# Sixteen-head attention on small tiles of TensorE: score halves on its rows, value groups on its columns, quotients taken transposed

## The chip, the cores and the metric

The kernel runs on one NeuronCore of a Trainium2 chip. A core has engines that run beside each other, each with its own in-order queue: TensorE (PE in the profile: matmuls, with PEld for the loads of its stationary operand), VectorE (DVE), ScalarE (ACT), GpSimd (POOL) and SyncE (SP, which issues DMAs). TensorE writes only to PSUM, whose banks hold 512 f32 columns on each of 128 partitions; the other engines read it from there. The metric is device time of one execution in microseconds; the median of several runs is compared.

## The reference: what is computed

A Flamingo-like block of four layers on x of shape (2, 1024, 256), with a context of 64 rows per batch. Each layer is a gated cross-attention to the context and a gated mixture of experts (8 experts, inner width 1024). Everything is f32. The change concerns the attention of layers L1 and L3, which have 16 heads of 16 columns. Cut to what matters (L3; L1 has a key mask that adds -10000 to masked scores in place of the full mask, and its keys are masked too):

```python
q = split_heads(query @ wq_kernel + wq_bias)          # (b, 16, 1024, 16)
k = split_heads(key @ wk_kernel + wk_bias)            # (b, 16, 64, 16)
v = split_heads(value @ wv_kernel + wv_bias)
scores = jnp.einsum('bhqd,bhkd->bhqk', q, k) / jnp.sqrt(jnp.float32(HD))
scores = jnp.where(m == 0, jnp.float32(-1000000000.0), scores)
attn = jax.nn.softmax(scores, axis=-1)
out = jnp.einsum('bhqk,bhkd->bhqd', attn, v)
return out @ wo_kernel + wo_bias                      # after joining the heads
```

The result is multiplied by a gate and added to x.

## The kernel before

The 2048 tokens stand in SBUF as 16 tiles of 128 tokens (`xs`), in four groups (`NG`) of four tiles (`TG`). The layers follow each other: `xattn0`, `moe0`, `middle`, the experts of L2, `heads_xattn(heads3)` for the attention of L3, the experts of L3. `middle` holds the attention of L1, its experts (`ffn1_group`) and the single-head attention of L2, group by group: the attention of L1 for groups 0 and 1 stands ahead of the experts of group 0; that for groups 2 and 3 is written after the experts of groups 0 and 1. A planner of the framework orders the instructions of each engine from the dependencies, so that attention and expert work are mixed in the engines' queues; it also makes the waits and hands out the buffers.

The class `Heads` does the attention of L1 and L3. `setup` makes two operands once: `kblk`, in which the scaled keys of eight heads (128 rows) stand block-diagonally against eight times 64 columns, and `vaug`, in which for each pair of heads the values stand in two column groups of 17: sixteen value columns and a column of ones, so that one matmul gives the weighted values and the sum of the weights together. Then for each group:

- `queries` makes `qT`, the transposed queries of the group's 512 tokens, in two chunks `c` of eight heads (L372, L373).
- `scores` takes one tile of 128 tokens: for each chunk one matmul (L386) with all 128 rows of `qT` as the stationary operand and 512 columns of `kblk` streaming gives the scores of eight heads in one PSUM bank. On DVE follow the mask (L394, in L3) or the added key bias, which moves the scores to SBUF (L401, in L1), the maximum of each head (L408) and the subtraction (L409). One exponential for all 1024 columns follows on ACT (L412).
- `values` transposes the weights on PE, two heads at a time (L425), ACT copies them to `pT` (`evac`, L145), and eight matmuls (L434) use `pT` as the stationary operand with 34 columns of `vaug` streaming. DVE takes 16 reciprocals a row (L442) and multiplies (L444).
- `output` transposes the result (L452), ACT copies it to `oT`, two matmuls with `wo` follow (L458, by the helper at L198), DVE adds to `xs` (L460), POOL adds the bias (L461).

`group` writes these for tile i, i-1 and i-2 in one turn of its loop (L466 to L472). PSUM buffers: in L3 and for group 0 of L1 there are two for transposes (`pt`), four for scores (`ps`) and two for the rest (`py`). For groups 1 to 3 of L1 the class `Both` (L1178) hands out the same two `py` buffers for all three uses, since the experts hold the other banks.

Of the kernel before, what the change touches and what calls it, by code (L numbers as in the profile page):

```python
# [8 lines left out]
F32 = mybir.dt.float32  # L9
# [8 lines left out]
P = 128  # L18
B, S, D = 2, 1024, 256
SK = 64  # L20
# [21 lines left out]
def kernel(ctx: ExitStack, tc: tile.TileContext, a: dict, out: bass.AP):  # L42
# [100 lines left out]
    def evac(i, dst, src):  # L143
        if i % 2:
            A.copy(dst, src)  # L145
        else:
            V.tensor_copy(dst, src)  # L147
# [143 lines left out]
    class Heads:  # L291
# [8 lines left out]
        def setup(self, psp, tag):  # L300

            pre, key_mask, full_mask = self.pre, self.key_mask, self.full_mask
            tmp = wpool.tile([P, 2048], F32, name="w")
            wk = tmp[:, :512].rearrange("p (c d) -> p c d", c=NC)
            wv = tmp[:, 512:1024].rearrange("p (c d) -> p c d", c=NC)
            nc.sync.dma_start(wk, a[f"{pre}_wk"])
            nc.sync.dma_start(wv, a[f"{pre}_wv"])
            self.wq, self.wo = (load_w256(held, f"{pre}_{n}", n) for n in ("wq", "wo"))

            kblk = self.kblk = held.tile([P, B, NC, P // HD, SK], F32, name="kblk")  # L310
            vaug = self.vaug = held.tile([P, B, H // 2, 2, HD + 1], F32, name="vaug")
            if key_mask is not None:
                km_u = held.tile([P, B * SK // 4], I32, name="km_u")
                nc.scalar.dma_start(
                    km_u, key_mask.rearrange("b k -> (b k)").partition_broadcast(P)
                )
                km = held.tile([P, B * SK], F32, name="km")
                V.tensor_single_scalar(km, km_u.bitcast(U8), 0.0, ALU.not_equal)
                self.kbias = held.tile([P, B * SK], F32, name="kbias")
                V.tensor_scalar(self.kbias, km, -1.0, 10000.0, ALU.add, ALU.mult)  # L320
            if full_mask is not None:
                m_w = wpool.tile([P, 2048], F32, name="w")
                m_i = m_w[:, : NT * SK].rearrange("p (t k) -> p t k", k=SK).bitcast(I32)
                nc.scalar.dma_start(
                    m_i, full_mask.rearrange("b (t p) k -> p (b t) k", p=P)
                )
                self.dropm = held.tile([P, NT, SK], U8, name="dropm")
                V.tensor_single_scalar(self.dropm, m_i, 0.0, ALU.is_equal)
            for c in range(NC):
                ps = psp.tile([P, 512], F32, name=tag)  # L330
                mm256(
                    ps[:, :P], lambda k: wk[:, k, c * P : (c + 1) * P], lambda k: ctxT[:, k, :]
                )
                kT = tmp[:, 1024 + c * P : 1024 + (c + 1) * P]
                V.tensor_scalar(
                    kT, ps[:, :P], cols[:, self.c_bk, c : c + 1], 1.0 / HD**0.5,
                    ALU.add, ALU.mult,
                )
                if key_mask is not None:
                    V.tensor_mul(kT, kT, km)  # L340
                for b in range(B):
                    V.tensor_mul(
                        kblk[:, b, c],
                        kT[:, b * SK : (b + 1) * SK].unsqueeze(1)
                        .to_broadcast([P, P // HD, SK]),
                        blkmask.unsqueeze(2).to_broadcast([P, P // HD, SK]),
                    )

            for b in range(B):
                ps = psp.tile([P, 512], F32, name=tag)  # L350
# [3 lines left out]
                V.tensor_mul(  # L354
                    vaug[:, b, :, :, 0:HD],
                    v2.rearrange("p (i j d) -> p i j d", j=2, d=HD),
                    halfmask.unsqueeze(1).unsqueeze(3).to_broadcast([P, H // 2, 2, HD]),
                )
# [19 lines left out]
        def scores(self, tt, pools):  # L378

            b, t = tt // (NT // B), tt % TG  # L380
            two, pss = pools["two"], pools["ps"]
            pr = two.tile([P, H, SK], F32, name="pr")
            HC = H // NC
            for c in range(NC):
                ps = pss.tile([P, 512], F32, name="ps_s")
                T.matmul(  # L386
                    ps,
                    lhsT=self.qT[:, c, t * P : (t + 1) * P],
                    rhs=self.kblk[:, b, c].rearrange("p j k -> p (j k)"),
                    start=True, stop=True,  # L390
                )
# [7 lines left out]
                prc = pr[:, c * HC : (c + 1) * HC, :]  # L399
                if self.key_mask is not None:  # L400
                    V.tensor_add(  # L401
                        prc, ps3,
                        self.kbias[:, b * SK : (b + 1) * SK].unsqueeze(1)
                        .to_broadcast([P, HC, SK]),
                    )
                    ps3 = prc
                mx = two.tile([P, HC], F32, name="mx")
                V.tensor_reduce(mx, ps3, AX.X, ALU.max)  # L408
                V.tensor_tensor(  # L409
                    prc, ps3, mx.unsqueeze(2).to_broadcast([P, HC, SK]), ALU.subtract  # L410
                )
            A.activation(pr, pr, AF.Exp)  # L412
            self.live[tt] = pr

        def values(self, tt, pools):

            b = tt // (NT // B)
            two, pt, py = pools["two"], pools["pt"], pools["py"]
# [10 lines left out]
                    )  # L429
                evac(1, pT[:, q4 * 4 : q4 * 4 + 4, :].rearrange("p i q -> p (i q)"), pst)  # L430
            pso = py.tile([P, 512], F32, name="ps_y")
            w = 2 * (HD + 1)
            for hp in range(H // 2):
                T.matmul(  # L434
                    pso[:, hp * w : (hp + 1) * w],
                    lhsT=pT[:, hp, :],
                    rhs=self.vaug[:, b, hp].rearrange("p a d -> p (a d)"),
                    start=True, stop=True,
                )
            po3 = pso[:, : (H // 2) * w].rearrange("p (h d) -> p h d", d=HD + 1)  # L440
            rs = two.tile([P, H], F32, name="rs")
            V.reciprocal(rs, po3[:, :, HD])  # L442
            o = two.tile([P, H, HD], F32, name="o")
            V.tensor_mul(o, po3[:, :, 0:HD], rs.unsqueeze(2).to_broadcast([P, H, HD]))  # L444
            self.live[tt] = o

        def output(self, tt, pools):
            two, pt, py = pools["two"], pools["pt"], pools["py"]
# [12 lines left out]
            G.tensor_add(xt, xt, self.bo)  # L461
# [864 lines left out]
```

## Time and profile before

| | us |
|---|---|
| three runs | 2466.1, 2443.22, 2464.13 (median 2464.13) |
| the profiled execution, whole | 2454.52 |
| its span, first to last instruction | 2452.7 |
| granted TensorE clock, mean of the span | 0.922 |

| stretch of the profiled execution | from, to (us) |
|---|---|
| L1 attention, group 0, by itself | 430 to 466 |
| L1 attention, group 1, with the experts of group 0 | about 480 to 520 |
| L1 attention, group 2, with the experts of group 1 | 806 to 850 |
| L1 attention, group 3, with the experts of group 2 | 1146 to 1190 |
| L3 attention, four groups | 2062 to 2206 |

The page gives busy time of each engine, then the chain of work that ended last, followed back from the last instruction, with each engine's share. A group of instructions is named by its line in the kernel, its engine, its tiles (what is written, an arrow, what is read) and its shape; for matmuls the shape of the stationary operand stands first (`128*34` would be 128 rows and 34 columns), then that of the streaming one. Busy time of TensorE covers the pipeline of overlapping matmuls, so the distance between starts tells more of a matmul's price than its duration.

### The profile page before, as it was taken

Reading aid. Unit: us, or ns where it says so; the run is one execution under the profiler, and the core shown is the slowest. Engines: PE = TensorE matmul, PEld = TensorE weight load, DVE = VectorE, ACT = ScalarE, POOL = GpSimd, SP = SyncE. Lnnn points to the kernel's source line nnn. Section 1 sums busy time; section 2 is a strip of 40 time slices with the busy share of each in tenths; the row PEclk is TensorE's granted clock in tenths of the full one; section 3 lists DMA queues with packets and bytes.
Section 4 is the critical chain, followed back from the end, with each engine's and each line's share of the span. In section 5 each row is a group of like instructions: output and inputs, shape, how many; then the busy total and the mean of one; then the engine's idle time right before and its main releaser. Section 6 shows DMA issues by size and latency. Waiting matters only on the chain.

```text
span 2452.7 us, 27852 instructions
## 1 busy us (share of the span) xinstructions
PE 2199.9 (90%) x10132; PEld 1787.2 (73%) x10132; DVE 1255.2 (51%) x2742; ACT 757.9 (31%) x1431; POOL 1072.5 (44%) x1229
## 2 busy tenths in 40 slices
PE   5558887899999999999999999999968996986997
PEld 3357775588888778887788887888856774565775
DVE  7851003676566765655865656566551116663111
ACT  1003332353333533334433334333311221330221
POOL 3316664236666346665366664666303320000331
PEclk9758998899999989999999999999958998875998
DMA  3018887012222123222132222222413543010442
GB/s 97 26 59 270 275 248 241 1 52 86 86 86 87 50 63 91 89 88 73 48 95 88 88 91 78 86 86 86 141 66 86 139 112 92 18 58 22 116 116 51
DMA packets 97544, 235.07 MB, mean 96 GB/s; under 512 B 13184, under 2 KB 41088, under 8 KB 86976
## 3 DMA queue, kind: packets, MB, share of 16 engines
q1 hardware_dynamic: 70880, 159.14, 20.3%
q0 software_dynamic: 21456, 68.92, 10.3%
q10 hardware_dynamic: 5072, 5.23, 0.6%
q8 instruction: 81, 1.33, 0.2%
q14 instruction: 55, 0.45, 0.1%
HBM read 211.10 MB, written 24.25 MB: 96 GB/s over the span
## 4 chain that ended last, share of the span: by engine, by line
PE 74%; DVE 11%; DMA 5%; POOL 3%; issue 2%; ACT 2%; POOLq 0%; ACTq 0%; DVEq 0%; SPq 0%
PE ps_b L1036 12%; PE ps_m L198 10%; PE ps_e L1036 8%; PE ps_a L1036 8%; PE ps_y L765 8%; PE ps_b L1081 6%; PE ps_a L1081 4%; PE ps_e L1081 4%; PE ps_y L198 3%; PE ps_y L434 2%; DMA xg<-hd,idx 2%; PE ps_m L704 1%; PE ps_tr L186 1%; DMA xd_L<-y_ff,idx 1%; PE ps_y L386 1%
## 5 line engine op out<-in xcount | busy, mean ns | idle before, releaser
L1036 PE MATMUL ps_b<-xsum,w 128*128 128x256 f32 x1536 | 388.2, 381 | 2.3 <-DVE c L1062 2.2
L1036 PEld LDWEIGHTS ps_b<-xsum,w 128*128 128x128 f32 x1536 | 289.7, 190 | 47.6 <-issue 4.6
L943 POOL TENSOR_TENSOR w<-w 128x256 f32<-128x256 f32 x192 | 140.8, 734 | 404.0 <-DMA w<-in_L_Wu_dram 174.6
L1036 PE MATMUL ps_a<-hT,w 128*128 128x256 f32 x1024 | 270.0, 384 | 0.7 <-DVE hT L147 0.6
L198 PE MATMUL ps_m<-xT,w 128*128 128x128 f32 (+2 forms) x1248 | 253.8, 364 | 11.8 <-DVE xT L147 11.7
L765 PE MATMUL ps_y<-w,mid 128*128 128x256 f32 (+1 forms) x1136 | 252.8, 379 | 0.0
L198 PEld LDWEIGHTS ps_m<-xT,w 128*128 128x128 f32 x1248 | 188.5, 200 | 71.9 <-DVE xT L147 19.3
L765 PEld LDWEIGHTS ps_y<-w,mid 128*128 128x128 f32 (+1 forms) x1136 | 206.6, 184 | 38.9 <-issue 2.7
L988 ACT COPY u<-ps_b 128x512 f32<-128x512 f32 (+1 forms) x192 | 98.9, 515 | 411.0 <-PE ps_b L1081 264.0
L1036 PEld LDWEIGHTS ps_a<-hT,w 128*128 128x128 f32 x1024 | 194.2, 193 | 31.2 <-issue 3.2
L772 POOL DMA_INDIRECT xd_L<-y_ff,idx x48 | 74.9, 1561 | 232.4 <-DVE y_ff L771 135.8
L770 DVE TENSOR_TENSOR y_ff<-ps_y,b 128x256 f32<-128x256 f32 (+1 forms) x48 | 20.3, 423 | 298.0 <-PE ps_y L765 298.0
L944 POOL TENSOR_TENSOR w<-w 128x256 f32<-128x256 f32 x192 | 166.9, 869 | 0.0
L946 POOL TENSOR_TENSOR w<-w 128x256 f32<-128x256 f32 x192 | 158.9, 827 | 14.7
L945 POOL TENSOR_TENSOR w<-w 128x256 f32<-128x256 f32 x192 | 164.8, 859 | 0.0
L1036 PE MATMUL ps_e<-xsum,w 128*128 128x256 f32 x512 | 134.4, 383 | 0.0
L1036 PE MATMUL ps_e<-hT,w 128*128 128x256 f32 x512 | 134.1, 382 | 0.0
L1081 PE MATMUL ps_b<-t,w 128*128 128x256 f32 x512 | 132.8, 384 | 0.0
L1081 PE MATMUL ps_a<-b,w 128*128 128x256 f32 x512 | 132.0, 379 | 0.0
L970 ACT COPY ps_b<-ps_a 128x512 f32<-128x512 f32 (+1 forms) x192 | 96.5, 502 | 109.5 <-DVE b L1066 63.5
L1098 POOL TENSOR_TENSOR m<-m,accT 128x256 f32<-128x256 f32 x60 | 71.7, 1195 | 124.1 <-ACT m L976 110.4
L145 ACT COPY xT<-ps_tr 128x128 f32<-128x128 f32 (+2 forms) x39 | 13.4, 344 | 355.7 <-PE ps_tr L748 289.4
(306 smaller groups left out, 3928.5 us busy)
## 6 DMA issues: line engine op xcount, KB each, us to landing
w<-in_L_Wg_dram SPq DMA_DIRECT2D x64, 512.0 KB, 4.1
w<-in_L_Wu_dram SPq DMA_DIRECT2D x64, 512.0 KB, 4.1
w<-in_L_Wd_dram SPq DMA_DIRECT2D x64, 512.0 KB, 3.7
w<-in_L_W_dram SPq DMA_DIRECT2D x32, 1024.0 KB, 4.9
xd_L<-xs SPq DMA_DIRECT2D x8, 512.0 KB, 2.9
hd_L<-h SPq DMA_DIRECT2D x8, 512.0 KB, 3.0
xs<-in_x_dram SPq DMA_DIRECT2D x4, 512.0 KB, 10.5
xd<-xs SPq DMA_DIRECT2D x4, 512.0 KB, 2.9
```

The costliest lines, as they stand in the source:

```text
L198: T.matmul(ps, lhsT=lhs(c), rhs=rhs(c), start=(c == 0), stop=(c == n - 1))
L765: T.matmul(ps[:w, :], lhsT=mid[:, f, at : at + w], rhs=w2[:, f, :], start=(f == 0), stop=(f == NF - 1),)
L772: G.indirect_dma_start(out=xd[:, :], out_offset=bass.IndirectOffsetOnAxis(ap=idx[:w, j0 + s : j0 + s + 1], axis=0), in_=y[:w, :], in_offse ...
L943: G.tensor_add(s[0], a21, a22)
L944: G.tensor_sub(s[1], s[0], a11)
L945: G.tensor_sub(s[2], a11, a21)
L946: G.tensor_sub(s[3], a12, s[1])
L970: A.copy(self.b, self.pa)
L988: A.copy(u2, self.b)
L1036: T.matmul(ps[:, q * 256 : (q + 1) * 256], lhsT=lhs[kind][:, q, :], rhs=xr[kind], start=(first and q == 0), stop=True, skip_group_check=True,)
L1081: T.matmul(ps, lhsT=wd[kind][:, q, :], rhs=m["rhs"][kind][:, q * 256 : (q + 1) * 256], start=(clear and q == 0), stop=True, skip_group_che ...
L1098: G.tensor_add(sb, sb, acc[:, i, j])
```

## The change

*Scores.* The two matmuls of a tile with all 128 rows become four with 64 rows each, one for each half `r` of the rows and chunk `c`. A half holds four heads, so only 256 columns of `kblk` stream. The results of half 0 go to one PSUM bank and those of half 1 to another, so a tile takes both banks at once. The softmax then runs over a half (both chunks) where it ran over a chunk. In L1 the key bias is added in place in PSUM. In L3 the subtraction is dropped: DVE takes the negated maximum, and ACT makes one exponential for each head, with that maximum as its bias.

*Values.* The operands change places: `vblk` (32 columns, two heads, no ones) is stationary and `pT` streams with 128 columns; four matmuls write four groups of 32 partitions of the same PSUM columns. The result comes out transposed. The sums of the weights come from the same matmuls with a new constant `halves` (ones for a head's half of the rows) as the stationary operand: 16 columns for each head hold the same sum. DVE takes reciprocals of 256 columns in two instructions and multiplies.

*Output.* Since the quotients are already transposed, the two transposes and the copy on ACT go.

```diff
+    halves = const.tile([P, 2, HD], F32, name="halves")
+    V.tensor_copy(halves, halfmask.unsqueeze(2).to_broadcast([P, 2, HD]))
...
-            vaug = self.vaug = held.tile([P, B, H // 2, 2, HD + 1], F32, name="vaug")
+            vblk = self.vblk = held.tile([P, B, H // 2, 2, HD], F32, name="vblk")
...
-                V.tensor_copy(
-                    vaug[:, b, :, :, HD],
-                    halfmask.unsqueeze(1).to_broadcast([P, H // 2, 2]),
                 )
...
+            prv = pr.rearrange("p (c r j) k -> p r c j k", c=NC, r=2)
             HC = H // NC
+            pair = [pss.tile([P, 512], F32, name="ps_s") for _ in range(2)]
             for c in range(NC):
-                ps = pss.tile([P, 512], F32, name="ps_s")
-                T.matmul(
-                    ps,
-                    lhsT=self.qT[:, c, t * P : (t + 1) * P],
-                    rhs=self.kblk[:, b, c].rearrange("p j k -> p (j k)"),
-                    start=True, stop=True,
-                )
-                ps3 = ps.rearrange("p (j k) -> p j k", k=SK)
+                for r in range(2):
+                    T.matmul(
+                        pair[r][:, c * 256 : (c + 1) * 256],
+                        lhsT=self.qT[r * 64 : (r + 1) * 64, c, t * P : (t + 1) * P],
+                        rhs=self.kblk[r * 64 : (r + 1) * 64, b, c, r * 4 : (r + 1) * 4]
+                        .rearrange("p j k -> p (j k)"),
+                        start=True, stop=True,
+                    )
+            for r in range(2):
+                ps3 = pair[r].rearrange("p (j k) -> p j k", k=SK)
+                ps4 = pair[r].rearrange("p (c j k) -> p c j k", c=NC, k=SK)
...
                 if self.key_mask is not None:
                     V.tensor_add(
-                        prc, ps3,
+                        ps3, ps3,
...
+                if self.full_mask is not None:
+                    V.tensor_reduce(mx, ps3, AX.X, ALU.max, negate=True)
+                    for j in range(HC):
+                        c, k = divmod(j, HC // NC)
+                        A.activation(
+                            prv[:, r, c, k], ps3[:, j], AF.Exp, bias=mx[:, j : j + 1]
+                        )
+                    continue
                 V.tensor_reduce(mx, ps3, AX.X, ALU.max)
                 V.tensor_tensor(
-                    prc, ps3, mx.unsqueeze(2).to_broadcast([P, HC, SK]), ALU.subtract
-                )
-            A.activation(pr, pr, AF.Exp)
+                    prv[:, r], ps4,
+                    mx.rearrange("p (c j) -> p c j", c=NC).unsqueeze(3)
+                    .to_broadcast([P, NC, HC // NC, SK]),
+                    ALU.subtract,
+                )
+            if self.full_mask is None:
+                A.activation(pr, pr, AF.Exp)
...
-            w = 2 * (HD + 1)
-            for hp in range(H // 2):
-                T.matmul(
-                    pso[:, hp * w : (hp + 1) * w],
-                    lhsT=pT[:, hp, :],
-                    rhs=self.vaug[:, b, hp].rearrange("p a d -> p (a d)"),
-                    start=True, stop=True,
-                )
-            po3 = pso[:, : (H // 2) * w].rearrange("p (h d) -> p h d", d=HD + 1)
-            rs = two.tile([P, H], F32, name="rs")
-            V.reciprocal(rs, po3[:, :, HD])
-            o = two.tile([P, H, HD], F32, name="o")
-            V.tensor_mul(o, po3[:, :, 0:HD], rs.unsqueeze(2).to_broadcast([P, H, HD]))
-            self.live[tt] = o
+            for at, den in ((D, True), (0, False)):
+                for c in range(NC):
+                    for i in range(4):
+                        w = halves if den else self.vblk[:, b, c * 4 + i]
+                        T.matmul(
+                            pso[i * 32 : (i + 1) * 32, at + c * P : at + (c + 1) * P],
+                            lhsT=w.rearrange("p a d -> p (a d)"),
+                            rhs=pT[:, c * 4 + i, :],
+                            start=True, stop=True, skip_group_check=True,
+                        )
+            rs = two.tile([P, D], F32, name="rs")
+            for c in range(NC):
+                cs = slice(c * P, (c + 1) * P)
+                V.reciprocal(rs[:, cs], pso[:, D + c * P : D + (c + 1) * P])
+            oT = two.tile([P, NC, P], F32, name="oT")
+            V.tensor_mul(oT.rearrange("p c q -> p (c q)"), pso[:, :D], rs)
+            self.live[tt] = oT
...
-            of = self.live.pop(tt).rearrange("p h d -> p (h d)")
-            pst = pt.tile([P, 512], F32, name="ps_tr")
-            for c in range(NC):
-                T.transpose(
-                    pst[:, c * P : (c + 1) * P], of[:, c * P : (c + 1) * P], ident
-                )
-            oT = two.tile([P, NC, P], F32, name="oT")
-            evac(1, oT.rearrange("p c q -> p (c q)"), pst[:, : NC * P])
+            oT = self.live.pop(tt)
```

More of the change, by code (lines that the diff above doesn't have):

```diff
@@ L354, in setup @@
                 V.tensor_mul(
-                    vaug[:, b, :, :, 0:HD],
+                    vblk[:, b],
                     v2.rearrange("p (i j d) -> p i j d", j=2, d=HD),
                     halfmask.unsqueeze(1).unsqueeze(3).to_broadcast([P, H // 2, 2, HD]),
-                )
-                V.tensor_copy(
-                    vaug[:, b, :, :, HD],
-                    halfmask.unsqueeze(1).to_broadcast([P, H // 2, 2]),
                 )
@@ L398, in scores @@
                     )
-                prc = pr[:, c * HC : (c + 1) * HC, :]
                 if self.key_mask is not None:
                     V.tensor_add(
-                        prc, ps3,
+                        ps3, ps3,
                         self.kbias[:, b * SK : (b + 1) * SK].unsqueeze(1)
@@ L405, in scores @@
                     )
-                    ps3 = prc
                 mx = two.tile([P, HC], F32, name="mx")
+                if self.full_mask is not None:
[6 more added lines that the diff above has]
+                    continue
                 V.tensor_reduce(mx, ps3, AX.X, ALU.max)
                 V.tensor_tensor(
-                    prc, ps3, mx.unsqueeze(2).to_broadcast([P, HC, SK]), ALU.subtract
-                )
-            A.activation(pr, pr, AF.Exp)
+                    prv[:, r], ps4,
+                    mx.rearrange("p (c j) -> p c j", c=NC).unsqueeze(3)
+                    .to_broadcast([P, NC, HC // NC, SK]),
+                    ALU.subtract,
+                )
+            if self.full_mask is None:
+                A.activation(pr, pr, AF.Exp)
             self.live[tt] = pr
@@ L431, in values @@
             pso = py.tile([P, 512], F32, name="ps_y")
-            w = 2 * (HD + 1)
-            for hp in range(H // 2):
-                T.matmul(
-                    pso[:, hp * w : (hp + 1) * w],
-                    lhsT=pT[:, hp, :],
-                    rhs=self.vaug[:, b, hp].rearrange("p a d -> p (a d)"),
-                    start=True, stop=True,
-                )
-            po3 = pso[:, : (H // 2) * w].rearrange("p (h d) -> p h d", d=HD + 1)
-            rs = two.tile([P, H], F32, name="rs")
-            V.reciprocal(rs, po3[:, :, HD])
-            o = two.tile([P, H, HD], F32, name="o")
-            V.tensor_mul(o, po3[:, :, 0:HD], rs.unsqueeze(2).to_broadcast([P, H, HD]))
-            self.live[tt] = o
-        def output(self, tt, pools):
-            two, pt, py = pools["two"], pools["pt"], pools["py"]
-            of = self.live.pop(tt).rearrange("p h d -> p (h d)")
-            pst = pt.tile([P, 512], F32, name="ps_tr")
-            for c in range(NC):
-                T.transpose(
-                    pst[:, c * P : (c + 1) * P], of[:, c * P : (c + 1) * P], ident
-                )
-            oT = two.tile([P, NC, P], F32, name="oT")
-            evac(1, oT.rearrange("p c q -> p (c q)"), pst[:, : NC * P])
+            for at, den in ((D, True), (0, False)):
[15 more added lines that the diff above has]
+            self.live[tt] = oT
+        def output(self, tt, pools):
+            two, py = pools["two"], pools["py"]
+            oT = self.live.pop(tt)
             psy = py.tile([P, 512], F32, name="ps_y")
```

## The prediction

> **What bounds the kernel now.** I read the page's head first, then its chain of work, then busy time by stage, then the shapes of the instructions that the change touches, then single stretches of the timeline.
>
> ```profile
> PE 2199.9 (90%) x10132; PEld 1787.2 (73%) x10132; DVE 1255.2 (51%) x2742; ACT 757.9 (31%) x1431; POOL 1072.5 (44%) x1229
> ...
> PE 74%; DVE 11%; DMA 5%; POOL 3%; issue 2%; ACT 2%; POOLq 0%; ACTq 0%; DVEq 0%; SPq 0%
> ```
>
> TensorE is busy for nine tenths and holds 74% of the chain. The touched code is a small part of it: 16 token tiles in L1 (group 0 at 430 to 466 us, group 1 near 480 to 520, groups 2 and 3 at 806 to 850 and 1146 to 1190) and 16 in L3 (2062 to 2206), about 310 us. The two kinds of group have different limits:
>
> ```profile
> 430.00:466.00 36.00, 31.25 (x149) 20.05 (x149) 22.58 (x52) 11.99 (x19) 11.51 (x17) 0.91 0.00 1
> 806.00:850.00 44.00, 43.73 (x231) 34.27 (x231) 31.25 (x66) 29.38 (x42) 11.05 (x14) 1.00 0.08 25
> ...
> 2100.00:2134.00 34.00, 30.70 (x146) 20.92 (x145) 22.13 (x49) 11.50 (x18) 2.90 (x4) 0.90 0.03 8
> ```
>
> (Columns: stretch, length, busy us of PE, PEld, DVE, ACT and POOL with counts, PE clock, DMA share, GB/s.) In L1 groups 1 to 3 the attention is mixed with expert work, and PE is busy for 43.73 of 44 us: a pass saved there is time saved, if DVE keeps up. In L1 group 0 and in L3 nothing fills the gaps: PE waits for softmax and softmax for PE, so latency counts. The instructions:
>
> ```profile
> L434 PE MATMUL ps_y<-vaug,pT 128*128 128x34 f32 x512 | 69.2, 285 | 4.0 <-ACT pT L145 4.0
> ...
> L760 ACT ACTIVATE mid<-ps_m,b1j 128x128 f32<-128x128 f32 x184 | 67.9, 369 | 37.3 <-PE ps_m L198 25.8
> ...
> L386 PE MATMUL ps_s<-kblk,qT 128*128 128x512 f32 x80 | 39.7, 610 | 5.3 <-DVE pr L409 5.3
> ...
> L412 ACT ACTIVATE pr<-pr 128x1024 f32<-128x1024 f32 x32 | 33.9, 1059 | 37.0 <-DVE pr L409 35.2 <-DVE o L444 1.6
> ...
> L267 DVE RECIPROCAL rden<-rden 128x512 f32<-128x512 f32 x8 | 26.7, 3340 | 0.0
> ...
> L442 DVE RECIPROCAL rs<-ps_y 128x16 f32<-128x16 f32 x32 | 8.2, 258 | 47.3 <-PE ps_y L434 47.2
> ```
>
> (After the bar: busy us in all, mean ns of one, idle us before and its releaser.) The values run 512 times for 32 tiles of 8 matmuls: an f32 matmul is two passes (a transpose is one). What a pass costs in a row is in the chain in order of time (start, length), and how narrow passes behave in the timeline:
>
> ```profile
> 2109.12 1.71 PE ps_y L434 x16
> ```
> ```profile
> 870.80 1.03 PE L1036 MATMUL ps_b<-xsum,w 128*128 128x256 f32 x4
> 871.76 1.89 PE L198 MATMUL ps_y<-hT,wqh 128*16 128x512 f32 x4
> 873.58 1.13 PE L1036 MATMUL ps_a<-hT,w 128*128 128x256 f32 x4
> ...
> 883.45 0.61 PE L592 MATMUL ps_y<-pT,vh 64*16 64x256 f32 x4
> ```
>
> A value pass costs 1.71/16 = 0.107 us though only 34 columns stream: its weight load is the bound. A 256-column pass takes 0.216 (four make 1.03 with the last one's 0.38), a 512-column one 0.43 (1.89 with the last one's 0.59). The last line is the key one: four passes of 256 columns on two 64-row halves took 0.61 us, the time of two, so halves run side by side.
>
> **What the skill says.** The Trainium skill, "TensorE: Matmul & The Clock Gate", section "Measured speedup vs the span model", gives 2.38 times for three column tiles; the trace agrees for rows (0.61 against 1.03), none of its instructions shows columns. "TensorEngine Tiling (Array Packing)", "Key Properties": changing the tiling mode drains TensorE. Agreed: 871.76 is 0.10 after the end of the fourth 0.216 at 871.66, and 873.58 again 0.10 after 873.48. "VectorE: DVE Perf Modes", "First, the fixed hardware budget": reciprocal is an iterated divide. Agreed: (3340-258)/496 = 6.2 ns a column, against 1.3 for the softmax's subtraction (L409, mean 671 ns for 512).
>
> **The change part by part**, per token tile unless said.
>
> *Scores.* Before: 2 matmuls x 2 passes x 0.43 = 1.72 us of PE. After: 8 passes of 256 columns in side-by-side pairs, 4 x 0.216 = 0.86. *Values.* Before 1.71. After: 16 matmuls x 2 = 32 passes of 128 columns (0.109 each, as transposes in a row start) in fours, 8 x 0.109 = 0.87; an estimate, no row shows it. Bounds: 3.5 if columns take turns; below 0.87 nothing, the columns must stream. *Output.* Two transposes go, 0.22. *Mode switches,* new: into and out of each of the two blocks, 4 x 0.10, plus a full weight load of 0.107 that no earlier pass can hide, three times (not into the narrow one): 0.7. Bounds 0 (where PE would wait anyway) and 1.5 (blocks split by other work). Sum: 2.43 against 3.65, so -1.2 us of PE.
>
> *Reciprocals.* 16 quotients a row become 256: two of 128 columns, each 258 + 112 x 6.2 = 950 ns, some 0.87 apart, in place of one of 258 ns (starts 0.17 apart): +1.57 us of DVE. The multiply stays. Behind them on DVE wait the residual of the tile before and the next softmax.
>
> *L3 softmax.* Two subtractions go from DVE, 2 x 0.60 (starts), so DVE gains only 0.37 in sum. ACT makes 16 exponentials of 64 columns: with the bias form of L760 (128 columns, 369) and of L373 (512 columns, mean 689) the slope is (689-369)/384 = 0.83 ns, so 316 ns each; ACT instructions in a row start about 0.10 sooner, 0.22, so 3.5 us (bounds 3.4 and 5.1) for 1.06. Behind them the pT copies wait. *Output copy* (oT, 373 ns on ACT): gone.
>
> *L1 softmax.* The same three DVE instructions, but the sum now stays in PSUM: a score buffer is held for all three (2.0 us) and not for one (0.69), and a tile takes two at once. In groups 1 to 3 there are only two buffers in all, shared with transposes, values and outputs. Cost 0 while expert work fills PE; bounds 0 and 3 us a group. The set-up (halves added, four small DVE copies gone) is under 1 us; nothing on SP's or POOL's queues moves.
>
> *Dense groups (12 tiles).* 12 x -1.2 = -14.8 (unrounded). Off it: in 806 to 850 DVE has 31.25 us and gets 4 x 1.57 more, 37.5 in some 39; near full, I charge 2 us a group for PE waiting, +6. Group 1 is followed by a wait for weights (3.84 us of DMA in the chain at 521.91), which takes half of its -4.9, +2.4. Sum -6.4.
>
> *L3 (4 groups of about 34 us).* Group 2100 to 2134: first softmax instruction 2101.45, last exponential done 2123.86, last output 2131.5. That phase of 22.4 becomes about 20: ACT needs 64 x 0.22 + 3 x 0.96 of pT = 17, starting 1.4 later, with 1.5 of waits; DVE needs 10 + 7.4. The tail loses transposes, copy and their hand-offs (1.07) and half a microsecond of values, and gets 1.6 of reciprocals: about even. -2 a group, -8.
>
> *L1 group 0.* DVE's phase (438.65 to 459.24) has some 3.5 us of slack for 3 tiles x 1.57 = 4.7; with waits +2.
>
> Sum -6.4 - 8 + 2 = **-12.4 us**. Durations are of the profiled execution (2454.5 us, span 2452.7), which lies 0.4% under the median of 2464.1 (runs 2443 to 2466). From the median 2451.7, from the mean of all four (2457.0) 2444.6; I say 2450.
>
> **The rivals.** *Gain everywhere:* DVE and ACT stay hidden, and all 32 tiles give 1.2 us: -39, so 2425. For it: PE's 74% of the chain; against: in the latency groups PE already waits. 0.22.
> *Reciprocals and held buffers bound L1 (slower):* if DVE is over about 95% busy in the attention stretches, or PE waits for the two score buffers, the PE saving turns into waiting, and 16 x 1.57 = 25 in L1 plus 16 x 0.37 = 6 in L3 is exposed: 2464 + 31 = 2495. For it: 37.5 of 39 us; against: expert work of 300 us follows into which attention can spread. 0.15.
> *Columns take turns (slower):* the two passes of a matmul use the same columns, so in strict order four groups may overlap little. Values 3.5: +1.8 - 0.86 - 0.22 + 0.7 = +1.4 a tile, +17 dense and as much for the other 20 tiles, half hidden, +14: 2495. It decides from about 2.2 us a tile. Against: the halves in the 0.61 line overlap with two passes each. 0.12.
> That score halves find their buffers at different times and don't pair loses 0.86 on 12 tiles and lies within the forecast.
>
> **How the numbers follow.** Forecast 0.51, alone 2432 to 2472 (ACT and DVE bounds, run spread). A measurement tells about 1%, 24.6 us, from no change. Faster: 0.2 of the first rival and 0.14 of the forecast's lower end, 0.34. Slower (over 2489): 0.6 of the slower rivals, 0.17. Same 0.49. Range 2416 to 2490.
>
> **What would show it.** Right: scores of 8 passes in about 0.9 us, 32 value passes in 0.9 to 1.1, reciprocals near 950 ns, 64-column exponentials starting 0.22 apart, L3 groups near 32 us, DVE over 80% in the dense stretches with PE still over 95%. Wrong: value passes starting 0.1 apart, PE idle for DVE in 806 to 850, L3 groups over 36 us.

## The result and the profile after

The change takes 2442.71 us (median of 20 runs, 2433.64 to 2449.09) against 2459.43 us before (20 runs on the same chip): ratio 0.9944, 95% interval 0.9931 to 0.9956, some 14 us less. (The quotient of the two medians alone is 0.9932, or 17 us, at the edge of that interval.) The profiled execution took 2447.51 us, its span 2445.7.

The page's head and the first line of its chain of waits:

```profile
PE 2176.5 (89%) x10708; PEld 1756.1 (72%) x10708; DVE 1276.5 (52%) x2739; ACT 777.8 (32%) x1637; POOL 1067.4 (44%) x1229
...
PE 72%; DVE 11%; DMA 5%; POOL 4%; issue 3%; ACT 2%; POOLq 0%; DVEq 0%; ACTq 0%; SPq 0%
```

PE has 23 us less work and two points less of the chain; DVE has 21 us more and keeps its 11%. The groups by shape:

```profile
L463 DVE RECIPROCAL rs<-ps_y 128x128 f32<-128x128 f32 x64 | 56.6, 924 | 17.9 <-PE ps_y L454 17.8
L417 ACT ACTIVATE pr<-ps_s,mx 128x64 f32<-128x64 f32 x256 | 54.2, 378 | 14.2 <-DVE mx L414 13.9
L389 PE MATMUL ps_s<-kblk,qT 64*128 64x256 f32 x160 | 41.1, 515 | 4.3 <-DVE pr L422 2.4 <-ACT pr L417 1.3
L454 PE MATMUL ps_y<-pT,halves 128*32 128x128 f32 x512 | 27.2, 313 | 7.7 <-ACT pT L148 7.0 <-DVE xs L474 0.5
L454 PE MATMUL ps_y<-pT,vblk 128*32 128x128 f32 x512 | 22.4, 297 | 0.0
L389 PE MATMUL ps_y<-kblk,qT 64*128 64x256 f32 x96 | 20.1, 404 | 0.0
```

The reciprocals take 924 ns (950 forecast). The values and the sums together are 1024 passes and yet keep PE busy for only 50 us, where the 512 passes before took 69 us: they do run side by side. For the score passes these rows don't tell, since their durations overlap; the distance between their starts does. The timeline of the L1 attention of group 2 shows both, and a new wait (start, length, first instruction's line, count; in brackets the idle time before):

```profile
829.08 1.13 PE L389 MATMUL ps_y<-kblk,qT 64*128 64x256 f32 x4
...
832.93 1.13 PE L389 MATMUL ps_y<-kblk,qT 64*128 64x256 f32 x4
...
837.68 0.65 PE L454 MATMUL ps_y<-pT,halves 128*32 128x128 f32 x16
838.14 0.62 PE L454 MATMUL ps_y<-pT,vblk 128*32 128x128 f32 x16
838.83 1.77 DVE L463 RECIPROCAL rs<-ps_y 128x128 f32<-128x128 f32 x2 [0.25 <-PE ps_y L454]
...
841.91 1.14 PE L389 MATMUL ps_y<-kblk,qT 64*128 64x256 f32 x8
...
845.47 1.28 DVE L406 TENSOR_TENSOR ps_y<-ps_y,kbias 128x512 f32<-128x512 f32 x2
845.70 1.13 PE L1050 MATMUL ps_b<-xsum,w 128*128 128x256 f32 x4
846.66 1.28 DVE L421 TENSOR_REDUCE mx<-ps_y 128x8 f32<-128x512 f32 x2
847.85 1.28 DVE L422 TENSOR_TENSOR pr<-ps_y,mx 128x512 f32<-128x512 f32 x2
848.68 1.22 PE L443 MATMUL ps_y<-ident,pr 128*128 128x128 f32 x8 [1.85 <-DVE pr L422]
```

The 32 value passes of one tile start within 0.81 us and end after 1.08. Eight score passes that find both buffers free take 1.14 (841.91), the same as four at 829.08: there one half of a tile had its buffer, and the other half followed only at 832.93, for another 1.13. In the whole trace 144 of the 256 score passes start beside another (7 ns apart, 14 at most); most of the others are 216 ns or more apart. And at 848.68 the transposes of the tile before waited for one of the two PSUM buffers, held by the score halves through three DVE instructions (`l1_release` below bears it out): PE, busy for nearly all of this stretch before, stood still for 1.85 us. This is one of the signs that the prediction had named as wrong, "PE idle for DVE in 806 to 850". The stretches that answer to those shown before (stretch, length, busy us of PE, PEld, DVE, ACT and POOL, PE clock, DMA share, GB/s):

```profile
444.00:480.00 36.00, 28.09 (x215) 16.76 (x214) 27.28 (x55) 9.99 (x14) 4.62 (x7) 0.78 0.00 1
813.00:857.00 44.00, 41.37 (x286) 30.83 (x284) 36.05 (x66) 26.63 (x38) 8.11 (x11) 1.00 0.11 34
2099.00:2133.00 34.00, 28.30 (x216) 17.26 (x215) 23.94 (x50) 18.64 (x74) 2.91 (x4) 0.80 0.04 13
```

In the dense stretch DVE went from 31.25 to 36.05 us and PE from 43.73 to 41.37, that is 94% of the 44 us.

**Stages.** The first 429 to 445 us differ between runs by 16 us though no kernel changes more in them than a few instructions of set-up, so I compare stages by their marks: L1 group 0 (first query to last residual), the three dense groups in sum (from there to the experts' end of groups 0, 1 and 2), L3 (first query to last residual), and from there to the first expert output. One profiled execution each, in us; what each kernel changes stands with the experiments below:

| kernel | ratio to before (95%) | L1 group 0 | dense | L3 | after L3 | PE clock in L3 |
|---|---|---|---|---|---|---|
| before | 1 | 30.7 | 1002.6 | 145.5 | 74.4 | 0.86 |
| the change | 0.9944 (0.9931-0.9956) | 34.2 | 992.0 | 141.0 | 69.7 | 0.83 |
| v_only | 0.9961 (0.9947-0.9976) | 31.9 | 1005.3 | 138.0 | 69.3 | 0.93 |
| s_only | 1.0142 (1.0114-1.0169) | 40.2 | 996.9 | 165.3 | 72.4 | 0.71 |
| s_one_exp | 1.0085 (1.0054-1.0116) | 37.1 | 999.2 | 162.5 | 74.0 | 0.72 |
| s_l1 | 1.0013 (0.9998-1.0028) | 37.1 | 998.8 | 136.9 | 72.4 | 0.94 |
| l3_one_exp | 0.9962 (0.9944-0.998) | 33.4 | 996.0 | 142.5 | 73.8 | 0.88 |
| l1_chunks | 0.9957 (0.9943-0.997) | 32.8 | 1000.3 | 140.3 | 69.7 | 0.83 |
| l3_chunks | 0.9927 (0.9902-0.9952) | 33.5 | 995.6 | 138.0 | 69.2 | 0.93 |
| l1_release | 0.9941 (0.992-0.9961) | 35.8 | 999.4 | 139.5 | 69.8 | 0.88 |
| pair_bank | 0.9968 (0.9955-0.9982) | 41.0 | 995.4 | 141.2 | 71.2 | 0.89 |
| recip2 | 1.0158 (1.0126-1.0189) | 41.9 | 1015.3 | 165.5 | 65.8 | 0.78 |
| recip_none | 0.9895 (0.9863-0.9927) | 31.5 | 995.8 | 131.8 | 72.3 | 0.83 |
| recip_act | 1.0136 (1.0104-1.0168) | 36.7 | 1011.2 | 160.4 | 70.8 | 0.87 |

How far such a row can be trusted is seen where code is the same. The dense groups with the change's L1 took 992.0, 996.0, 995.6 and 995.4; but those of v_only and l1_chunks, whose L1 code is the same too, took 1005.3 and 1000.3. So one profile is good to some 2 to 5 us there. L3 of s_l1 is that of before, and took 136.9 and not 145.5, at a clock of 0.94 and not 0.86; so a difference of a few us in L3 is not told by one profile, and I go by the ratios. The spread between runs also goes with the clock: of 116 executions of the kernel before, those with a mean clock of 0.919 had a median of 2458.6 us, those with 0.926 of 2448.7.

For the dense groups I count, from the starts of PE's instructions, each pass by the distance at which passes of its width start in a row at full clock (0.109, 0.216 or 0.43 us; a pass beside another counts nothing), and what is over as waiting, put down to the pass that waited (time at a halved clock counts as waiting too). Attention passes: 75.7 us before, 57.2 in the change, so 18.5 saved. Waits ahead of attention passes: 3.7 before, 15.3 in the change (scores 0.8 and 3.5, transposes of weights 0.7 and 6.8, values 1.5 and 3.0, output 0.4 and 2.0). So 11.6 us of the 18.5 come back at once in front of the passes that were made cheaper.

That leaves 6.9 us, and the dense groups gained 10.6. The rest is in PE's other waits, ahead of expert passes, and what fell there is the time at a halved clock. The traces show the granted clock at 1 or at one half, for 3.4 us or a multiple. One such stretch of before, and the expert passes at its start:

```profile
887.00:897.20 10.20, 10.20 (x23) 7.24 (x23) 3.97 (x8) 2.35 (x4) 3.45 (x5) 0.50 0.33 103
...
887.10 2.08 PE L1036 MATMUL ps_b<-xsum,w 128*128 128x256 f32 x4
```

Four such passes take 2.08 us where at 870.80 they took 1.03. In the dense groups the clock stood at one half for this long, in us:

| kernel | time at half clock in the dense groups |
|---|---|
| before | 27.3 |
| new values alone (v_only, l1_chunks) | 32.6, 23.0 |
| halves alone (s_only, s_one_exp, s_l1) | 9.1, 10.2, 10.2 |
| both (the change, l3_one_exp, l3_chunks, pair_bank) | 11.4, 17.0, 13.6, 18.8 |

An estimate from these figures: a busy PE loses half of such a stretch, so before lost up to 13.7 us and the kernels with both 5.7 to 9.4, a difference of 4 to 8 us. That is more than half of the dense gain of each of the four, and the forecast had no term for it. In the dense groups of before, each of five gaps of PE of 1.3 us or more was followed by such a stretch, which began 2.3 to 3.8 us after the gap did; in the change only one of four was. So idle PE has to do with it, but no run shows what decides.

### The profile page after: what moved, and what is told of

It is laid out like the page before. It is cut to its first block, busy times and chain, and to the rows that moved or that the text cites. A ratio compares the mean times of both kernels' runs of the same rounds, so it can differ in the third digit from the quotient of the medians.

```text
span 2445.7 us, 29220 instructions
## 1 busy us (share of the span) xinstructions
PE 2176.5 (89%) x10708; PEld 1756.1 (72%) x10708; DVE 1276.5 (52%) x2739; ACT 777.8 (32%) x1637; POOL 1067.4 (44%) x1229
## 3 DMA queue, kind: packets, MB, share of 16 engines
q1 hardware_dynamic: 70880, 159.14, 20.4%
q0 software_dynamic: 21456, 68.92, 10.3%
## 4 chain that ended last, share of the span: by engine, by line
PE 72%; DVE 11%; DMA 5%; POOL 4%; issue 3%; ACT 2%; POOLq 0%; DVEq 0%; ACTq 0%; SPq 0%
PE ps_b L1050 13%; PE ps_m L201 10%; PE ps_e L1050 8%; PE ps_a L1050 8%; PE ps_y L779 8%; PE ps_b L1095 6%; PE ps_e L1095 4%; PE ps_a L1095 4%; PE ps_y L201 2%; DMA xg<-hd,idx 1%; PE ps_m L718 1%; DVE st L157 1%; DMA xd<-y_ff,idx 1%; PE ps_y L454 1%; PE ps_s L389 1%
## 5 line engine op out<-in xcount | busy, mean ns | idle before, releaser
L201 PE MATMUL ps_m<-xT,w 128*128 128x128 f32 (+2 forms) x1248 | 260.3, 370 | 18.3 <-DVE xT L150 17.8
L201 PEld LDWEIGHTS ps_m<-xT,w 128*128 128x128 f32 x1248 | 193.6, 205 | 79.8 <-DVE xT L150 25.5
## 6 DMA issues: line engine op xcount, KB each, us to landing
xs<-in_x_dram SPq DMA_DIRECT2D x4, 512.0 KB, 10.6
```

Source lines behind the costliest of these rows:

```text
L201: T.matmul(ps, lhsT=lhs(c), rhs=rhs(c), start=(c == 0), stop=(c == n - 1))
```

## The experiments

### Each half of the change alone

`v_only` keeps `scores` of the kernel before. `s_only` and `s_one_exp` keep `values` and `output` of the kernel before and have the new `scores`; `s_one_exp` goes without the exponentials per head.

```diff
 # v_only: the change, but
-    for r in range(2): T.matmul(pair[r][:, c * 256 : (c + 1) * 256], ... 64 rows ...)
+    T.matmul(ps, lhsT=self.qT[:, c, t * P : (t + 1) * P], rhs=self.kblk[:, b, c] ...)
```

> Values, quotients and output as in the change, scores and softmax as before, in L1 and L3. Theory 1 (the gain in the dense L1 groups comes from the values alone, since most score halves do not pair): 1.71 + 0.22 us of PE become 0.87 + 0.3 for the switches, so 0.75 us on 12 dense tiles, -9 us; L3 has its subtractions back beside the long reciprocals, so its -4.5 us is lost; in all -6 to -11 us against the kernel before (ratio 0.9955 to 0.9975). Rival (scores and values share the gain evenly): the same sum here, -8, but then the other half must show in the run with the scores alone.

> Score halves and their softmax as in the change, values, quotients and output as before. Theory 1: in L1 nothing is gained, since few halves pair and two buffers are held (0 to +4 us); in L3 DVE loses 1.2 us a tile and ACT gets 2.2, -2 to -5 us; in all within 4 us of the kernel before (ratio 0.998 to 1.001). Rival: about half of the change's gain, -8 us (0.9965).

The new values alone bring -0.39%, within 6 to 11 us, but not where that expectation put them: nothing in the dense groups (1005.3, and 1000.3 in l1_chunks, against 1002.6), so that by what is left they lie in L3 and after it. The score halves alone make the kernel slower by 1.4%, 35 us, which neither theory had. In the dense groups they gain (996.9); the loss is in L1 group 0 (+9.5) and in L3 (+20). L3's window says how, before (first) and in s_only:

```profile
2059.30:2204.80 145.50, 129.36 (x596) 88.24 (x595) 100.05 (x249) 48.63 (x76) 10.98 (x15) 0.86 0.08 26
```
```profile
2069.20:2234.50 165.30, 150.80 (x662) 112.43 (x661) 85.05 (x216) 85.45 (x316) 10.84 (x15) 0.71 0.06 21
```

PE has fewer microseconds of passes, counted by these distances (89.3 against 97.5), and is busy for 21 us more: the clock fell from 0.86 to 0.71. PE isn't idle for longer (14.5 us of the stretch against 16.1). DVE is freed and ACT is up by 37 us. Two suspects, then: the exponentials per head on ACT, and the halves themselves. Two kernels part them.

```diff
 # s_one_exp: s_only, but in L3
-    V.tensor_reduce(mx, ps3, AX.X, ALU.max, negate=True); for j ...: A.activation(..., AF.Exp, bias=mx[:, j : j + 1])
+    V.tensor_reduce(mx, ps3, AX.X, ALU.max); V.tensor_tensor(prv[:, r], ps4, mx ..., ALU.subtract); A.activation(pr, pr, AF.Exp)
 # s_l1: s_only, but L3 calls the scores function of the kernel before
```

> Scores in halves as in the change, but in L3 with the subtraction on DVE and one exponential; values, quotients and output as before the change. Theory (what made L3 20 us longer with new scores and old values is ACT: 16 exponentials a tile ahead of the pT and oT copies that the old values wait for): L3 back to 143 to 148, ratio 0.996 to 1.001. Rival (it is the score halves themselves: two buffers held through three DVE operations, passes that don't pair): L3 at 158 or above, ratio 1.010 or more.

> Score halves in L1 alone; L3 and all values, quotients and outputs as before the change. Theory (halves save PE passes in the dense groups, some 4 us of 1002.6 in the two runs with halves and old values, and what made those two slower was L3, where their granted clock was 0.71 and 0.72): L3 back at 144 to 147 with a clock of 0.84 or more, dense groups at 996 to 1000 in sum, L1 group 0 at 35 to 40, ratio 0.997 to 1.003. Rival (the low clock in L3 was not the halves': it follows the old values' longer blocks and what ran before): L3 at 155 or above with a clock under 0.8, ratio 1.006 or more.

One exponential takes back a part of the loss at most (1.0085 against 1.0142, and the two intervals touch), less than the theory asked for and just more than the rival's 1.010 allowed. L3 stays at 162.5 with a clock of 0.72, as the rival had it, so ACT is the smaller part at most. With full rows in L3 the loss is gone (1.0013), and of s_l1's theory all but the size of L3 came out. L3 of s_l1:

```profile
2063.30:2200.20 136.90, 119.20 (x598) 80.28 (x597) 99.96 (x250) 48.43 (x76) 10.98 (x15) 0.94 0.08 26
```

It is the score halves in L3, with the old values behind them, that lose the clock. Why halves should lower it isn't settled: no run changes the clock alone. All that the table shows is an order, of one profile each: full rows 0.86 to 0.94, halves with the new values 0.83 to 0.89 (0.78 in recip2), halves with the old ones 0.71 and 0.72. This trace of s_l1 is from the low end of its runs (2446 to 2464), so its 136.9 is no gain of the kernel; the ratio is what counts.

### Parts taken back in the full change

```diff
 # l3_one_exp: the change with subtraction and one exponential in L3, as in s_one_exp
 # l1_chunks:  the change; scores over full rows in L1
 # l3_chunks:  the change; scores over full rows, subtraction and one exponential in L3
```

> The whole change, but in L3 DVE subtracts the maximum and ACT makes one exponential of 1024 columns, as before. Theory 1: DVE in L3 then has 2.5 + 1.2 + 2.5 us a tile, over 24 us a group, and becomes its bound; L3 is 5 to 10 us longer than with the change, in all -7 to -12 us against the kernel before (0.995 to 0.997). Rival (64 short exponentials hold the score buffers and ACT bounds L3's first half): -17 us or better, L3 no longer than with the change.

> The whole change, but in L1 the scores are again two matmuls with all rows, the key bias moves them to SBUF, and a score buffer is freed after one DVE instruction. Theory 1 (unpaired halves and two held buffers cost PE waits in the dense groups, 7.5 us of PE gaps a group where there were 1.6): 3 to 8 us better than the change, -20 to -25 us against the kernel before (0.990 to 0.992). Rival (the row halves still pay in L1): worse than the change, -8 to -14 us.

> L1 as in the change (scores in halves, new values and quotients); in L3 the scores over all 128 rows, subtraction on DVE and one exponential as before, with the new values. Theory (the parts act stage by stage, and in L3 the score halves with their 64-column exponentials cost some 3 us against full rows: 141.0 in the change, 138.0 with the new values alone): dense groups as in the change, L3 near 138, ratio 0.991 to 0.994, about 3 us below the change. Rival (the difference of 3 us in L3 is the spread of single profiles, or the values gain only by what the halves leave): L3 at 141 or above, ratio 0.994 to 0.997.

`l3_one_exp` is 0.9962. That is inside the theory's ratio, but not by its reason: L3 is 1.5 us longer than in the change and not 5 to 10. The move from DVE to ACT is worth 0.4% at most, and perhaps nothing (the intervals of both ratios overlap). `l1_chunks` is 0.9957, and its dense groups take 1000.3 where the change's code takes 992.0 to 996.0: so the halves pay in the dense groups, although only 60 of the 128 score passes of L1 pair (for the whole kernel 0.9957 and 0.9944 have intervals that overlap). With s_only, s_one_exp and s_l1 (996.9, 999.2, 998.8) a square for the dense groups results, as means of two to four profiles: before 1002.6; new values alone 1002.8; halves alone 998.3; both 994.8. The values' 13.1 us of passes saved (62.6 against 75.7) are worth nothing by themselves and some 3.5 us beside the halves, hardly more than the spread. Nor are the halves' 4.3 us simply their 3.7 us of passes: the three kernels with halves alone are also at half clock for some 17 us less than before, and no run parts the two.

`l3_chunks` has L3 at 138.0 as expected, and 0.9927, the lowest ratio of all kernels that compute the whole. The interval of the change (0.9931 to 0.9956) overlaps, so all that is shown is that full rows in L3 lose nothing that these runs can tell.

### The reciprocals, doubled, left out, and on ACT

```diff
 # recip2
+    for _ in range(2):
         V.reciprocal(rs[:, cs], pso[:, D + c * P : D + (c + 1) * P])
 # recip_none
-    V.reciprocal(...);  V.tensor_mul(oT, pso[:, :D], rs)
+    V.tensor_mul(oT, pso[:, :D], ones_d)
 # recip_act: l3_chunks with
-    V.reciprocal(...)
+    A.activation(rs, pso[:, D : 2 * D], AF.Ln); A.activation(rs, rs, AF.Exp, scale=-1.0)
```

> The change with every reciprocal done twice: 1.74 us more of DVE per tile, 28 us in L1 and 28 us in L3. Theory (reciprocals lie on the path where PE has nothing else, and beside expert work in the dense groups): L3 longer by 12 to 28 us, L1 group 0 by 3 to 7, dense groups by 2 each at most; ratio to before 1.002 to 1.012. Rival one (DVE bounds the dense groups as well, so that the change's third dense group lost its gain to reciprocals): dense groups longer by 5 us each or more, ratio over 1.012. Rival two (hidden everywhere): ratio below 0.998.

> The change without its reciprocals: the values are multiplied by a constant tile of ones, so the division by the row sums is left out (the 16 passes that make the sums still run). Theory (a tile's 1.74 us of reciprocals lie on the path nearly whole, as doubling them cost 52 us of 56): 40 to 55 us less than the change, ratio 0.973 to 0.979, L3 at 116 to 125, each dense group 6 to 10 shorter. Rival (only the second copy of each was exposed; one copy lies beside PE and ACT work): at most 20 us less than the change, ratio 0.986 or above.

> L1 as in the change, L3 scores over full rows with one exponential, and the quotients made on ACT as exp(-ln(sum)), two activations of 256 columns, in place of DVE's two reciprocals. Theory (DVE's reciprocals are what gives the PE saving back, and ACT has room, 43 us of 138 in L3): about 0.95 us of ACT for 1.74 us of DVE, 15 to 35 us under the kernel with full rows in L3, ratio 0.979 to 0.987. Rival (on ACT the quotients queue with exponentials and copies, and tables change between ln and exp at 1.28 us each): two loads a tile would be 2.6 us, ratio 0.995 to 1.015.

Doubling costs 0.0214 of 2460.7, some 53 us (by the intervals 44 to 61), where 64 more reciprocals at 0.87 take 55.7 us; rival one had the size. Its dense groups are 20.5 us longer than the mean of the four with the change's L1, for 12 tiles times 1.74 = 20.9. From that I concluded that the first copy lies on the path as well, and expected 40 to 55 us from leaving it out. It gave 12 (0.9895 against 0.9944; by the intervals 4 to 20), and in the dense groups nothing (995.8); the rival was right again, and rival one's reason, that reciprocals had eaten the gain of the third dense group, is not borne out.

The likeliest reading is that DVE in the dense groups stands at an edge: the 1.74 us a tile that the change adds fill its slack, and what comes on top shows. It isn't shown apart from two other things. The planner orders both kernels anew, so that 6 pairs of score passes find each other in their dense groups and not 18 as in the change; and they are at half clock there for 25.0 us (recip2) and 20.4 (recip_none), where the four have 11.4 to 18.8. **A sensitivity taken on one side of the present point need not hold on the other side.**

On ACT the quotients are slower by 2% than on DVE. The rows, by shape:

```profile
L501 ACT ACT_TABLE_LOAD x32 | 41.1, 1283 | 0.6
L502 ACT ACT_TABLE_LOAD x27 | 34.6, 1283 | 0.5
L502 ACT ACTIVATE rs<-rs 128x256 f32<-128x256 f32 x32 | 13.2, 414 | 0.3
L501 ACT ACTIVATE rs<-ps_y 128x256 f32<-128x256 f32 x32 | 12.3, 383 | 13.5 <-PE ps_y L494 13.3
```

The two activations cost 0.8 us (0.95 expected); the tables changed 106 times in place of 31, 59 of them here, and 1283 ns each stood in the chain between sums and product.

### Buffers and pairing

```diff
 # l1_release: the key bias's sum goes to SBUF (pr), maximum and subtraction work there
-    V.tensor_add(ps3, ps3, self.kbias[...])
+    V.tensor_add(prv[:, r], ps4, self.kbias[...])
 # pair_bank: in L3 and L1 group 0, both halves in one buffer
-    pair = [pss.tile([P, 512], F32, name="ps_s") for _ in range(2)]     # 4 buffers
+    both = pss.tile([P, 2, 512], F32, name="ps_s"); pair = [both[:, 0, :], both[:, 1, :]]     # 2 buffers
```

> The change, but in L1 the key bias's sum goes to SBUF, so that a score buffer is free after one DVE operation (0.75 us) and not after three (2.1 us). Theory (held buffers keep the halves apart in time and make the waits of PE in L1): more than the 16 tiles' 144 of 256 score passes start beside another, waits of PE in the dense groups shrink by 2 us a group, L1 group 0 by 2 or more; from the first L1 query to the end 6 to 10 us less than in the change. Rival (the order in which the planner issues the passes and the length of the softmax chain on DVE decide, not when a buffer comes free): pairs as before, and within 3 us of the change.

> The change with both score halves of a tile in one buffer of two banks in L3 and L1 group 0 (two such buffers instead of four of one bank), so that a tile's four matmuls are issued together. Theory (the passes that don't pair cost L3 PE time and make waits): nearly all L3 passes start beside another, L3 at 136 to 138, L1 group 0 shorter by 1 to 2 us. Rival (L3 is bound by the chain through DVE, ACT and the reciprocals, and a joint buffer comes free later): L3 at 140 to 146, ratio within 0.002 of the change.

In `l1_release` the wait that the buffers made is gone, as its timeline shows at the place that answers to 845.47 to 848.68:

```profile
841.41 1.27 DVE L406 TENSOR_TENSOR pr<-ps_y,kbias 128x512 f32<-128x512 f32 x2
...
842.22 1.16 PE L443 MATMUL ps_y<-ident,pr 128*128 128x128 f32 x8
842.60 1.26 DVE L421 TENSOR_REDUCE mx<-pr 128x8 f32<-128x512 f32 x2
```

The transposes start while DVE is in the two instructions of L406, not after the first subtraction. Waits ahead of transposes fall from 6.8 us to 2.9, those of all attention passes from 15.3 to 10.8. The time doesn't: dense 999.4, ratio 0.9941. Nor do more halves pair: 120 of the 256 passes, where the theory had forecast more than 144. PE's other waits, in the expert work, rose to 40.4 us from 28.7 to 31.6 in the four runs with the change's L1. The theory had the wait right, the rival the time. The same happens in v_only: 7.2 us of waits ahead of attention, 45.1 elsewhere. A part of these other waits is the clock (20.4 us at half clock in l1_release, 32.6 in v_only, so at most half of that); the rest would be attention that ends earlier and meets expert work that isn't ready earlier. Which chain holds that up, the runs don't tell.

In `pair_bank` nearly all of L3's score passes pair (62 pairs of 64; 42 in the change). The row that was 41.1 us at 515 ns in the change:

```profile
L393 PE MATMUL ps_s<-kblk,qT 64*128 64x256 f32 x160 | 30.1, 472 | 5.3 <-DVE pr L426 4.7
```

L3 takes 141.2 all the same, as the rival had it; the ratio is 0.0024 above that of the change, just over the 0.002 that the rival allowed. L1 group 0 is 6.8 us longer; that a joint buffer comes free only when both halves are done would explain it, but wasn't tried apart. Pairing saves PE time in a stage that doesn't lack it.

## Why the prediction held, step by step

The sum was -12.4 us; the ratio gives -14 (-11 to -17). The stages of the table, from L1's first query on: L1 group 0 +3.5, dense -10.6, L3 and what follows it -9.2. The total came out, but not term by term: the parts below miss in both directions, and that they cancel is in part luck.

- **Dense and latency groups have different limits.** Right that they differ. But "a pass saved there is time saved" failed: v_only saved 13.1 us of passes in the dense groups and none of the time.
- **Values, 0.87 us for 32 passes in fours.** Right: 0.81. So the rival that columns take turns is out.
- **Score halves, 0.86 us in pairs.** A pair costs that, but 112 of 256 passes find no partner. The saving in the dense groups was 5.4 us in the change (57.2 of attention passes, 62.6 with the new values alone), and 3.7 in s_l1 (72.0 against 75.7), not 12 times 0.86 = 10.3. This was named as lying within the forecast, and is the largest wrong term of the pass count: 18.5 saved, 23.0 forecast before mode switches.
- **Mode switches, 0.7 us a tile.** The waits ahead of scores, values and output grew by 2.7 + 1.5 + 1.6 = 5.8 us over 12 tiles, 0.5 a tile. That holds waits of every kind on the way into these blocks, and nothing of the way out of them, so the term is not measured by itself; its size fits. (The forecast's parts as printed give 12 times -1.22 = -14.6 us, not -14.8; nothing hangs on it.)
- **Reciprocals: 6 us of PE waiting in the dense groups.** The instructions were priced right (924 ns, 0.87 apart); the term was wrong as far as recip_none shows: without them the dense groups are no shorter. Near full is not yet over full.
- **Held score buffers: cost 0, bounds 0 to 3 us a group.** Wrong value inside the bounds: the transposes waited 6.1 us more, 2 a group. This fills the place of the reciprocals' 6 us, and the shorter time at half clock (4 to 8 us, by the estimate above) makes up for the passes that didn't pair. So the stage's sum (-6.4; mean of four runs -7.9) came out right by luck as much as by its reasons. Releasing the buffers earlier moved the waits and not the time.
- **Half of group 1's gain goes into the weights' wait.** Not seen: the means of the four runs are -4.3 in the first dense group, -5.1 in the second, and +1.6 in the third (from -0.1 to +3.2), which kept nothing. Why the third didn't, the runs don't tell.
- **L1 group 0, +2.** +3.0 (mean of 34.2, 33.4, 33.5). The cause fits too: without the reciprocals it is 31.5, only 0.8 above before.
- **L3, -8.** -4.5 inside, which is less than the 8.6 us by which two profiles of the same L3 code differ, and -4.7 behind it. PE's passes fell by 26.5 us (97.5 to 71.0), and its waits rose by 15.7. In this pair of traces the part behind is the router's: in the chain in order of time, before and in the change,

```profile
2211.00 3.25 PE ps_m L198 x28
2215.45 6.64 PE ps_m L198 x32
2222.19 0.30 DVE r_pr L628
```
```profile
2207.27 1.51 PE ps_m L201 x8
2209.30 1.08 PE ps_m L201 x6
2211.90 3.60 PE ps_m L201 x16
2215.59 0.30 DVE r_pr L642
```

  60 router passes of the chain stood behind the last tile, now 30: the others run in PE's gaps in L3 (5.8 us of passes other than attention there, 2.2 before). The forecast had looked for the gain in each group's phases. It isn't seen in every kernel with the new values: l3_one_exp takes 73.8 us there, near the 74.4 of before. The exponentials came as forecast (0.195 us apart, 0.22 forecast), and one for all does no worse.
- **The rivals.** Gain everywhere (2425): no, waits ate over half. Reciprocals and held buffers turn it slower: held buffers do make waits, and recip2 suggests how near DVE's edge was; at the change's own cost the kernel is still the faster one.

## What to carry to other kernels

Before splitting a matmul into pieces that run side by side, look at who hands out their buffers: pieces that get them one by one run one by one, and each holds its buffer longer. A cheaper pass is worth what the waits behind it leave; count passes, waits and time at a lowered clock apart, since a saved pass can come back as a wait in the next place that isn't ready. To find out whether an operation lies on the path, take it away as well as double it: here doubling said 53 us and removal 12.

## What the runs showed of the hardware that was not expected

The granted clock is a term of the same size as the change. The kernel before, over 116 executions, ran with a mean clock from 0.917 to 0.932 and in 2469.8 to 2439.3 us. In the latency-bound L3 the clock differed from kernel to kernel (0.71 to 0.94), and from profile to profile of the same L3 code (0.86 and 0.94). There fewer PE passes went with a slower kernel: s_only had 8 us less of passes and 21 us more of busy PE. Even in the dense groups, where PE is nearly always busy, the time at half clock ran from 9 to 33 us by kernel. So an edit's passes can't simply be summed where the clock moves with it; it has to be timed.
